# Two transformer layers on one core: the first layer's modulation, routing and order of work rebuilt

## The chip, the cores and the metric

The kernel runs on one core of a Trainium2 chip. The metric is the time of one execution on the device in microseconds (us): the median of three runs is 1533.65, the lowest 1533.04, the highest 1539.41. A core has five engines with instruction streams of their own: PE (matrix products; the profile shows its weight loads as PEld), DVE (vector), ACT (activation functions), POOL (GpSimd, which also issues the indirect DMAs) and SP (which issues most plain DMAs). They meet at semaphores.

## What is computed

Two layers over x of 4 batches x 1024 tokens x 256 features, all in float32. Each layer takes six modulation vectors per batch from a small product, `silu(c) @ wmod`.

```
mod = silu(c) @ wmod                 -> sa, ca, ga, sb, cb, gb   (per batch; ga, gb kept away from 0)
x = x + ga * attn(layernorm(x) * (1 + ca) + sa)
x = x + gb * ffn (layernorm(x) * (1 + cb) + sb)
```

In the first layer `attn` is attention without softmax, so it can be written with the 256x256 gram matrix of a batch's rows: h times (masked gram, combiners, queries). Its `ffn` is a mixture of eight experts (256 -> 1024 -> 256, relu). A router (256 -> 8) picks the two best experts of each token, and their outputs are added with softmax weights. The second layer has a gated MLP whose weights decay from chunk to chunk, and a second mixture of eight experts.

## The kernel before

A tile is 128 tokens; a batch has NC = 8 tiles. The program has three stages.

1. **Attention and routing of the first layer**, batch by batch (lines 509 to 638). `modulation` (L177) makes the six vectors and spreads them over all partitions by products with a selector (L214) and copies. `attention_in(b)` normalises eight tiles (`normalise`, L225: statistics on DVE at L231, a square root on ACT at L236, the rows on ACT at L247), multiplies by the scale on DVE (L522), adds the shift on POOL (L523), transposes four tiles at a time on PE (`transpose4`, L256; evicted on ACT at L257), and forms the gram matrix (L546) and the small head products (L556, L568) that give a 128x128 masked matrix `md`. `attention_out` (L589) multiplies and adds to x on DVE (L597). `route0` normalises again, modulates, transposes, makes the router's logits (L617), stores the rows to DRAM, and calls `top2` and `Group.add`.
2. **The experts** (L641 to L728). The 8192 (token, expert) pairs are sorted by expert and cut into J = 71 blocks of 128. For each block POOL gathers the expert's weight rows (nothing moves where the expert stays the same) and the 128 input rows `xg`; PE transposes them (L655), multiplies by W1 (L671), ACT applies the relu (L678), PE multiplies by W2 (L690), DVE adds the bias (L698), SP stores the block to y0. At block 4 the second layer's modulation is made (again L188, L214, L221, L222).
3. **The second layer** (L731 on), chunk by chunk.

**The pair table.** `Group.add` ranks each pair within its expert (two float16 products, L368 and L369) and builds, for each of a tile's two choices, a 128x128 one-hot table scaled by the token's number (`g_at`, L391). `Group.close` counts the blocks of each expert, and 64 products of `g_at` with a one-hot over blocks (`g_which`, L472; L479) add up to the table `row`, which says which token stands at each place of each block. `wrow` holds the weight rows of a block, with an out-of-range number where the expert is the one already there.

**The order of the work.** A scheduler orders each engine's instructions at compile time from estimated costs; the source order only ranks them. Tiles live in pools with a fixed number of buffers, and an instruction waits for its buffer's last reader. The PSUM pools are `ps_1` (3 buffers), `ps_2` (2) and `ps_m` (3). The indirect DMAs stand in POOL's stream (L499), the plain ones in SP's or ACT's.

Of the kernel before, what the change touches and what calls it, by code (L numbers as in the profile page):

```python
# [8 lines left out]
F32 = mybir.dt.float32  # L9
# [4 lines left out]
AX = mybir.AxisListType  # L14
PSUM = bass.MemoryType.PSUM
DRAM = bass.MemoryType.DRAM

P = 128
# [19 lines left out]
def adaln_d2_kernel(  # L38
# [46 lines left out]
    nc.scalar.dma_start(c0, c0T)  # L85

    def load_x(b):
        nc.sync.dma_start(x_sb[:, :, b, :], x_in[b].rearrange("(c p) d -> p c d", p=P))

    load_x(0)  # L90

    poolA = tc.tile_pool(name="poolA", bufs=2)
    pa = poolA.__enter__()

    def load_mod(pool, wmod):
        w = pool.tile([P, KD, 6 * D], F32, name="wmod", bufs=1)
        for piece in range(3):
            cut = slice(piece * 2 * D, (piece + 1) * 2 * D)
            nc.scalar.dma_start(
                w[:, :, cut], wmod[:, cut].rearrange("(k p) n -> p k n", p=P)  # L100
            )
        return w

    wm0 = load_mod(pa, wmod0)
    qT = pa.tile([P, KD, 4, 64], F32, name="qT", bufs=1)
    comb = pa.tile([P, KD, 4, 64], F32, name="comb", bufs=1)
    load_x(1)
    nc.scalar.dma_start(comb, comb_in)
    nc.scalar.dma_start(qT, qT_in)
    load_x(2)  # L110
    load_x(3)
    wr_sb = const.tile([P, KD, E], F32, name="wr_sb")
    rw_sb = const.tile([P, KD, E], F32, name="rw_sb")
    br_sb = const.tile([P, E], F32, name="br_sb")
    for dst, src in ((wr_sb, WrT), (rw_sb, rwT), (c1, c1T)):
        nc.scalar.dma_start(dst, src)
    nc.scalar.dma_start(br_sb, br.partition_broadcast(P))
# [42 lines left out]
    def iota(name, pattern, shape, base=0, mult=0):  # L160
        i = const.tile(shape, I32, name=f"{name}_i")
        nc.gpsimd.iota(i, pattern=pattern, base=base, channel_multiplier=mult)
        f = const.tile(shape, F32, name=name)
        nc.gpsimd.tensor_copy(f, i)
        return f
# [5 lines left out]
    steps = iota("steps", [[P, NC * B]], [P, NC * B])  # L171

    token0 = iota("token0", [[P, NC * B]], [P, NC * B], base=-2048, mult=1)
# [3 lines left out]
    def modulation(scratch, layer, cT, w, names):  # L177

        sT = small.tile([P, KD, B], F32, name=f"sT{layer}")
        nc.scalar.activation(sT, cT, AF.Silu)  # L180
        rows = scratch.tile([B, 6, D], F32, name="mod_rows", bufs=1)
        tiles = []
        for i, (where, name) in enumerate(names):
            tiles.append(where.tile([P, B, D], F32, name=f"{name}{layer}", bufs=1))
        for piece in range(3):
            pr = psum(ps_m, [B, 2, D], "pm_mod")
            for k in range(KD):
                nc.tensor.matmul(  # L188
                    pr,
                    lhsT=sT[:, k, :],  # L190
                    rhs=w[:, k, piece * 2 * D : (piece + 1) * 2 * D],
                    start=(k == 0),
                    stop=(k == KD - 1),
                )
            for i in range(2):
                kind = (2 * piece + i) % 3
                dst = rows[:, 2 * piece + i, :]
                if kind == 0:
                    nc.scalar.copy(dst, pr[:, i, :])
                elif kind == 1:  # L200
                    nc.vector.tensor_scalar(dst, pr[:, i, :], 1.0, None, ALU.add)
                else:

                    sign = scratch.tile([B, D], F32, name="g_sign", bufs=1)
                    nc.vector.tensor_scalar(sign, pr[:, i, :], 0.0, 2.0, ALU.is_ge, ALU.mult)
                    size = scratch.tile([B, D], F32, name="g_size", bufs=1)
                    nc.vector.scalar_tensor_tensor(
                        size, sign, -1.0, pr[:, i, :], ALU.add, ALU.mult
                    )
                    nc.vector.tensor_scalar(size, size, 0.25, None, ALU.max)  # L210
                    nc.vector.scalar_tensor_tensor(dst, sign, -1.0, size, ALU.add, ALU.mult)
            for b in range(B):
                pb = psum(ps_m, [P, 2, D], "pm_bc")
                nc.tensor.matmul(  # L214
                    pb,
                    lhsT=pick[:, b, :],
                    rhs=rows[:, 2 * piece : 2 * piece + 2, :],
                    start=True,
                    stop=True,
                )  # L220
                nc.scalar.copy(tiles[2 * piece][:, b, :], pb[:, 0, :])  # L221
                nc.vector.tensor_copy(tiles[2 * piece + 1][:, b, :], pb[:, 1, :])  # L222
        return tiles
# [274 lines left out]
    def gather(dst, table, index, bound=None):  # L498
        nc.gpsimd.indirect_dma_start(  # L499
# [8 lines left out]

    gb0_pool = const
    sha0, sca0, ga0, shb0, scb0, gb0 = modulation(  # L510
        pa,
        0,
        c0,
        wm0,
        [(pa, "sha"), (pa, "sca"), (pa, "ga"), (pa, "shb"), (pa, "scb"), (gb0_pool, "gb")],
    )
    g0 = Group(const, "g0", NC * B, token0, pa)
    rows0 = dram.tile([B * NC * P, D], F32, name="rows0")
    hT_of = {}

# [4 lines left out]
    def attention_in(b):  # L525
        h = pa.tile([P, NC, D], F32, tag="h", name="h1")
        hT = pa.tile([P, KD, NC, P], F32, tag="hT", name="h1T")
        hT_of[b] = hT
        normalise([x_sb[:, c, b, :] for c in range(NC)], [h[:, c, :] for c in range(NC)])
        for g in range(NC // 4):  # L530
            cs = slice(4 * g, 4 * g + 4)
            modulate(
                h[:, cs, :],
                sca0[:, b, :].unsqueeze(1).to_broadcast([P, 4, D]),
                sha0[:, b, :].unsqueeze(1).to_broadcast([P, 4, D]),
            )
            transpose4(
                [h[:, c, :] for c in range(4 * g, 4 * g + 4)],
                lambda k: hT[:, k, cs, :],
            )  # L540

        gram = psum(ps_1, [P, KD, P], "pm_gram")
        for j in range(KD):
            for c in range(NC):
                hj = h[:, c, j * P : (j + 1) * P]
                nc.tensor.matmul(  # L546
                    gram[:, j, :], lhsT=hj, rhs=hj, start=(c == 0), stop=(c == NC - 1)
                )
        gd = pa.tile([P, KD, P], F32, tag="gd", name="gd")
        nc.gpsimd.memset(gd, 0.0)  # L550
        for r in (slice(0, 64), slice(64, P)):
            nc.vector.tensor_copy(gd[r, :, r], gram[r, :, r])
        t1 = pa.tile([P, KD, 4, 64], F32, name="t1")
        for j in range(KD):
            p1 = psum(ps_1, [P, 4 * 64], "pm_t1")
            nc.tensor.matmul(  # L556
                p1,
# [5 lines left out]
            nc.scalar.copy(t1[:, j, :, :].rearrange("p a g -> p (a g)"), p1)  # L563
# [12 lines left out]
        md = pa.tile([P, KD, P], F32, tag="md", name="md")  # L576
        nc.gpsimd.memset(md, 0.0)
# [3 lines left out]
        return md  # L581

    def attention_out(b, md):
        hT = hT_of[b]
        for c2 in range(NC // 2):
# [13 lines left out]
    def route0(b):  # L599
        h = pa.tile([P, NC, D], F32, tag="h", name="h2")  # L600
        hT = pa.tile([P, KD, NC, P], F32, tag="hT", name="h2T")
        normalise([x_sb[:, c, b, :] for c in range(NC)], [h[:, c, :] for c in range(NC)])
        pl = psum(ps_1, [P, NC, E], "pm_l")
        for g in range(NC // 4):
            cs = slice(4 * g, 4 * g + 4)
            modulate(
                h[:, cs, :],
                scb0[:, b, :].unsqueeze(1).to_broadcast([P, 4, D]),
                shb0[:, b, :].unsqueeze(1).to_broadcast([P, 4, D]),
            )  # L610
            transpose4(
                [h[:, c, :] for c in range(4 * g, 4 * g + 4)],
                lambda k: hT[:, k, cs, :],
            )
            for c in range(4 * g, 4 * g + 4):
                for k in range(KD):
                    nc.tensor.matmul(  # L617
                        pl[:, c, :],
                        lhsT=hT[:, k, c, :],
                        rhs=wr_sb[:, k, :],  # L620
                        start=(k == 0),
                        stop=(k == KD - 1),
                    )
        nc.sync.dma_start(
            rows0[b * NC * P : (b + 1) * NC * P, :].rearrange("(c p) d -> p c d", p=P), h
        )
        cut = slice(b * NC, (b + 1) * NC)
        top2(pl, br_sb, NC, g0.one[:, :, cut, :], g0.w[:, :, cut], None)
        g0.add(b * NC, NC)

    mds = {0: attention_in(0)}
    for b in range(B):
        if b + 1 < B:
            mds[b + 1] = attention_in(b + 1)
        attention_out(b, mds[b])
        route0(b)
    g0.close(2048, True)
# [10 lines left out]

    def fetch(work, table, index):
# [383 lines left out]
```

## Time and profile before

| quantity | value |
|---|---|
| median of three runs | 1533.65 us |
| the profiled execution | 1540.93 us, its span (first to last instruction) 1539.2 us |
| mean granted PE clock | 0.878 of full speed |
| busy time of PE, DVE, ACT, POOL | 1219.2, 536.8, 514.8, 611.5 us |
| first product of an expert | 234.7 us from the span's start |
| last expert block's add (L698) | 786.4 us |
| indirect DMAs of expert weights (L499, w) | 142, 994 ns each on POOL |

How to read a profile line: start, duration, engine, line of the kernel, operation, output <- inputs, shape, how many were merged, and in brackets how long the engine had been idle and what released it. In the list of windows, each engine has its busy time and, in brackets, its number of instructions. Products in float32 appear as two records, transposes as one.

### The profile page before, as it was taken

The page shows a single profiled execution, that of the slowest core. Times are in us where ns is not written, and L with a number is a line of the kernel's source. Part 1 is how long each engine was busy: PE and PEld are TensorE (multiplying, and loading weights), DVE is VectorE, ACT ScalarE, POOL GpSimd, SP SyncE. Part 2 cuts the span into 40 slices and gives each one's busy share as a digit, 9 for nine tenths or more (in the row PEclk, how much of TensorE's full clock was granted, in tenths as well). Part 3 has the DMA queues.
Part 4 walks back from the last instruction along what each step waited for, and adds up shares of the span by engine and source line. Part 5 has one row for each costly group of instructions (what it writes and reads, how often), then busy time and mean ns, then how long its engine had stood idle before and what let it go on. Part 6 is the DMA issues. An engine that isn't in the chain of part 4 may idle for free.

```text
span 1539.2 us, 17629 instructions
## 1 busy us (share of the span) xinstructions
PE 1219.2 (79%) x6137; PEld 920.1 (60%) x6137; DVE 536.8 (35%) x1719; ACT 514.8 (33%) x1153; POOL 611.5 (40%) x592
## 2 busy tenths in 40 slices
PE   4966449999999999999940679999988898724683
PEld 1566438599989999899930345565545464513341
DVE  5487560210101001100115645555652425152143
ACT  3254203234344443344322315544251423121121
POOL 3022213143334333443347841111244433687645
PEclk8766559799999999999975889999999999856786
DMA  7000024043242332414122210000124332535633
GB/s 281 1 28 28 30 70 171 14 151 112 77 152 65 127 119 67 155 38 152 32 59 72 69 34 14 14 14 1 39 62 129 92 100 76 153 113 166 169 114 101
DMA packets 81048, 133.18 MB, mean 87 GB/s; under 512 B 25760, under 2 KB 60704, under 8 KB 76864
## 3 DMA queue, kind: packets, MB, share of 16 engines
q0 software_dynamic: 38576, 83.90, 18.5%
q1 hardware_dynamic: 39744, 44.45, 8.4%
q10 hardware_dynamic: 2640, 3.70, 0.7%
q8 instruction: 49, 0.80, 0.2%
q14 instruction: 39, 0.32, 0.1%
HBM read 228.66 MB, written 30.54 MB: 168 GB/s over the span
## 4 chain that ended last, share of the span: by engine, by line
PE 49%; POOL 12%; issue 10%; DMA 10%; DVE 7%; ACT 3%; POOLq 0%; DVEq 0%; ACTq 0%
PE p_h L671 14%; PE p_y L690 13%; PE p_f L796 6%; POOL yg L499 5%; PE p_u L781 3%; DMA w<-in_W,g_wrow 3%; PE p_v L781 3%; DMA we<-in_ew,ga_wrow 2%; PE p_e L879 2%; DMA we<-in_ew,gb_wrow 2%; POOL h L523 2%; POOL x_sb L756 2%; POOL xg L499 2%; PE pm_x L655 1%; PE pm_t L256 1%
## 5 line engine op out<-in xcount | busy, mean ns | idle before, releaser
L678 ACT ACTIVATE hid<-p_h,w 128x128 f32<-128x128 f32 x568 | 208.2, 367 | 341.8 <-PE p_h L671 322.8
L671 PEld LDWEIGHTS p_h<-xT,w 128*128 128x128 f32 x2272 | 298.0, 193 | 19.9 <-DVE xT L657 6.7
L690 PE MATMUL p_y<-w,hid 128*128 128x256 f32 x1136 | 299.7, 381 | 5.3 <-DMA w<-in_W,g_wrow 5.3
L671 PE MATMUL p_h<-xT,w 128*128 128x128 f32 x2272 | 303.1, 277 | 0.6 <-DVE xT L657 0.5
L499 POOL DMA_INDIRECT w<-in_W,g_wrow x142 | 141.1, 994 | 326.7 <-ACT hid L678 228.8
L690 PEld LDWEIGHTS p_y<-w,hid 128*128 128x128 f32 x1136 | 192.2, 192 | 22.1 <-DMA w<-in_W,g_wrow 3.8
L698 DVE TENSOR_TENSOR y<-p_y,w 128x256 f32<-128x256 f32 x71 | 30.2, 425 | 466.6 <-PE p_y L690 460.3
L879 PE MATMUL p_e<-we,xT 128*128 128x256 f32 x280 | 91.4, 462 | 78.1 <-DMA we<-in_ew,gb_wrow 43.9
L781 PE MATMUL p_v<-h3T,a 128*128 128x512 f32 x256 | 131.6, 628 | 15.2 <-ACT hf L789 15.2
L781 PE MATMUL p_u<-h3T,a 128*128 128x512 f32 x256 | 130.5, 624 | 4.6 <-DVE hf L790 3.8
L879 PEld LDWEIGHTS p_e<-we,xT 128*128 128x128 f32 x280 | 58.5, 227 | 112.6 <-issue 49.5
L256 PE MATMUL pm_t<-ident,h 128*128 128x128 f32 x256 | 45.0, 331 | 90.4 <-POOL h L523 90.2
L796 PE MATMUL p_f<-a,hf 128*128 128x256 f32 x512 | 114.4, 382 | 0.0
L796 PEld LDWEIGHTS p_f<-a,hf 128*128 128x128 f32 x512 | 97.7, 192 | 17.5 <-issue 4.5
L657 DVE COPY xT<-pm_x 128x256 f32<-128x256 f32 x141 | 56.3, 419 | 143.6 <-PE p_e L879 113.3
L256 PEld LDWEIGHTS pm_t<-ident,h 128*128 128x128 f32 x256 | 37.0, 175 | 102.0 <-POOL h L523 99.7
L781 PEld LDWEIGHTS p_v<-h3T,a 128*128 128x128 f32 x256 | 48.4, 200 | 68.1 <-issue 43.6
L499 POOL DMA_INDIRECT xg<-rows,g_row x71 | 68.4, 963 | 50.0 <-PE pm_x L655 22.5
L523 POOL TENSOR_TENSOR h<-h,shb 128x1024 f32<-128x1024 f32 x16 | 38.4, 2399 | 115.2 <-DVE h L522 85.0
L781 PEld LDWEIGHTS p_u<-h3T,a 128*128 128x128 f32 x256 | 48.8, 200 | 55.7 <-issue 42.9
L887 ACT COPY y<-p_e 128x256 f32<-128x256 f32 x70 | 26.0, 371 | 159.4 <-PE p_e L879 156.4
L499 POOL DMA_INDIRECT yg<-y,g_slot x64 | 66.1, 1033 | 32.7 <-issue 29.0
(228 smaller groups left out, 1527.2 us busy)
## 6 DMA issues: line engine op xcount, KB each, us to landing
y<-y SPq DMA_DIRECT2D x71, 128.0 KB, 1.7
ga_y<-y SPq DMA_DIRECT2D x39, 128.0 KB, 2.1
x_sb<-in_x SPq DMA_DIRECT2D x4, 1024.0 KB, 13.1
rows<-h SPq DMA_DIRECT2D x4, 1024.0 KB, 4.5
out_x<-x_sb SPq DMA_DIRECT2D x8, 512.0 KB, 2.9
gb_y<-y SPq DMA_DIRECT2D x31, 128.0 KB, 2.2
wmod<-in_wmod ACTq DMA_DIRECT2D x6, 512.0 KB, 9.4
a<-in_fw SPq DMA_DIRECT2D x3, 1024.0 KB, 10.9
```

The source lines that it names most:

```text
L256: nc.tensor.transpose(pt[:, i, :], src[i][:, k * P : (k + 1) * P], ident)
L499: nc.gpsimd.indirect_dma_start(out=dst, out_offset=None, in_=table, in_offset=bass.IndirectOffsetOnAxis(ap=index, axis=0), bounds_check=bound,
L523: nc.gpsimd.tensor_tensor(h, h, shift, ALU.add)
L657: nc.vector.tensor_copy(xT, pt)
L671: nc.tensor.matmul(p1[:, i, :], lhsT=w1[:, k * H + m * P : k * H + (m + 1) * P], rhs=xT[:, k, :], start=(k == 0), stop=(k == KD - 1),)
L678: nc.scalar.activation(hid[:, m, :], p1[:, i, :], AF.Relu, bias=w1[:, KD * H + m : KD * H + m + 1],)
L690: nc.tensor.matmul(p2, lhsT=hid[:, m, :], rhs=w2[:, m * D : (m + 1) * D], start=(m == 0), stop=(m == KH - 1),)
L698: nc.vector.tensor_tensor(y, p2, w2[:, KH * D :], ALU.add)
L756: nc.gpsimd.tensor_tensor(x_sb[:, c, :, :], x_sb[:, c, :, :], sum_, ALU.add)
L781: nc.tensor.matmul(ps, lhsT=a[:, k, m * P : (m + 1) * P], rhs=hT[:, k, :, :], start=(k == 0), stop=(k == KD - 1),)
L796: nc.tensor.matmul(p2, lhsT=hid[m][:, b * P : (b + 1) * P], rhs=a1[:, m, :], start=(m == 0), stop=(m == KH - 1),)
L879: nc.tensor.matmul(p2, lhsT=xT[:, k, :], rhs=we[:, k * D : (k + 1) * D], start=(k == 0), stop=(k == KD - 1),)
```

## The change

It rewrites the first stage and touches the other two only where they take something from it.

- **Modulation at the eviction.** The shift and scale of the first layer are made with features on the partitions (`mods_by_feature`). The normalised rows are transposed first; ACT's eviction of the transposes applies scale and shift as per-partition operands (`to_features`). Where token-major rows are needed (gram, rows in DRAM), PE transposes back and ACT copies (`to_tokens`). The multiply on DVE and the add on POOL are gone.
- **Pair numbers by indirect DMA.** The class `Regions` takes the place of `Group` in the first layer. Each expert has a region of 4096 places in a DRAM table. After a batch is ranked, one indirect DMA per tile and choice writes 128 pair numbers of 4 bytes to their places: 64 DMAs in all. At the end one gather of 71 lines of 128 numbers reads the table back in blocks. It waits for all the scatters. `g_at`, `g_which` and their products are gone. The softmax weights and slots are computed later, at block 4 of the experts (`weights`).
- **A fixed order.** Inside `tc.manual_schedule` the instructions of PE, ACT, DVE and POOL keep the source order, and the source weaves the first attention half of batch b+1 into the second half of batch b. The last batch is routed in two halves. x is loaded in halves.
- **The second layer's modulation** is multiplied out at the end of the first stage (`modulation1`) and spread at expert block J-8 (`spread1`).
- **Rows two blocks ahead.** `xg` of block j+2 is gathered ahead of the weights of block j.

The core of the diff (`-` before, `+` after):

```
+    def to_features(b, src, n0, dst, d0, shift, scale):
+        for k in range(KD):
+            pt = psum(ps_m, [P, 4, P], "pm_t")
+            for i in range(4):
+                nc.tensor.transpose(pt[:, i, :], src[:, n0 + i, k * P : (k + 1) * P], ident)
+            nc.scalar.activation(dst[:, k, d0 : d0 + 4, :], pt, AF.Identity,
+                bias=modT[:, shift, k, b : b + 1], scale=modT[:, scale, k, b : b + 1])
...
+        def scatter(self, s):
+            for i in range(2):
+                nc.gpsimd.indirect_dma_start(
+                    out=self.table.rearrange("r l -> (r l)").unsqueeze(1),
+                    out_offset=bass.IndirectOffsetOnAxis(ap=self.index[:, i, s : s + 1], axis=0),
+                    in_=self.pair[:, i, s : s + 1], ...)
...
-    mds = {0: attention_in(0)}
-    for b in range(B):
-        if b + 1 < B:
-            mds[b + 1] = attention_in(b + 1)
-        attention_out(b, mds[b])
-        route0(b)
-    g0.close(2048, True)
+    with tc.manual_schedule(engines=ORDERED):
...
+        for b in range(B):
+            last = b == B - 1
+            for g in range(2):
+                attention_out(b, g)
+                if b and g:
+                    g0.ranks()
+                norm2(b, g)
+                if not last:
+                    features1(b + 1, g)
+                if b and g:
+                    g0.places()
+                    for q in range(2):
+                        scatter(b - 1, q)
+                if not last:
+                    tokens1(b + 1, g)
+            if not last:
+                gram(b + 1)
+                pl = psum(ps_1, [P, NC, E], "pm_l")
+                features2(b, 0)
+                t1 = head_t1(b + 1)
+                router(b, 0, pl[:, :4, :])
+                features2(b, 1)
+                head_m(b + 1, t1)
+                tokens2(b, 0)
+                router(b, 1, pl[:, 4:, :])
+                if b + 2 < B:
+                    for g in range(2):
+                        norm1(b + 2, g)
+                tokens2(b, 1)
+                g0.route(pl, br_sb, b * NC, NC)
+            else:
+                sT1 = silu_of(1, c1)
+                for g in range(2):
+                    features2(b, g)
+                    pl = psum(ps_1, [P, 4, E], "pm_l")
+                    router(b, g, pl)
+                    if g:
+                        g0.ranks()
+                        g0.places()
+                        scatter(b, 0)
+                    tokens2(b, g)
+                    g0.route(pl, br_sb, b * NC + 4 * g, 4)
+                modulation1(sT1, wm1, 0)
+                g0.ranks()
+                g0.places()
+                scatter(b, 1)
+                g0.total()
+                modulation1(sT1, wm1, 1)
+                g0.close(pa, lambda: modulation1(sT1, wm1, 2))
...
     def expert_in(j):
         w1 = w1buf[j % 2]
+        if j + 2 < g0.J:
+            xg_of[j + 2] = rows_of(work, rows0, g0.row[:, j + 2 : j + 3])
         gather(w1, W1, g0.wrow[:, j : j + 1], E * P - 1)
         gather(w2buf[j % 2], W2, g0.wrow[:, j : j + 1], E * P - 1)
-        xT = fetch(work, rows0, g0.row[:, j : j + 1])
+        xT = turned(work, xg_of.pop(j))
...
         if j == 4:
-            sha1, sca1, ga1, shb1, scb1, gb1 = modulation(work, 1, c1, wm1, ...)
+            g0.weights(work)
+            for i in (2, 5):
+                gate_of(rows1[:, i, :], rows1[:, i, :], work)
+        if j == g0.J - 8:
+            sha1, sca1, ga1, shb1, scb1, gb1 = spread1(l1)
```

The functions named in the loop: `attention_out(b, g)` the products of half a batch with `md` and the add to x; `norm1` and `norm2` the normalisation of half a batch (four tiles) for attention and for routing, without modulation; `features1` and `features2` call `to_features`; `tokens1` and `tokens2` call `to_tokens`, the latter also stores the rows; `gram`, `head_t1` and `head_m` the parts of the old `attention_in`; `route` the two best experts; `ranks` up to nine float16 products; `places` the place numbers from them.

## The prediction

> **What bounds it now.** I read the page's slices first, to see which stage belongs to which part of the program, then the chain that ended last for the stage's end, then the windows and the time line inside it. Times are microseconds from the span's start.
>
> ```profile
> PE   4966449999999999999940679999988898724683
> ...
> PEclk8766559799999999999975889999999999856786
> ```
>
> A slice is 38.5 us. Six uneven slices hold the first layer's attention and routing; then PE is full for fourteen, in all but one at a granted clock of 0.9 or more (the 71 expert blocks, to 786.4); the second layer follows. The diff leaves the second layer's instructions in the same order on all engines, so I cost it at nothing. What is at stake is when the experts start, and what the experts lose on the way. The chain at the seam:
>
> ```profile
> 218.62 6.35 issue
> 225.01 0.51 issue
> 225.55 0.19 issue
> 225.73 7.73 DMA xg<-rows,g_row
> 233.55 0.68 PE pm_x L655 x2
> 234.25 0.44 DVE xT L657
> 234.73 2.93 PE p_h L671 x12
> ```
>
> The pair table is closed, the first rows are gathered (7.73, beside 5 MB of weight loads issued at 224.7), and at **234.7** the experts begin. Inside the stage no engine is full for long:
>
> ```profile
> core 0: us, PE busy (x) PEld busy (x) DVE busy (x) ACT busy (x) POOL busy (x), PEclk, DMA share, GB/s
> 75.00:100.00 25.00, 16.14 (x72) 14.86 (x72) 20.72 (x71) 13.40 (x25) 7.37 (x4) 0.62 0.13 43
> 100.00:125.00 25.00, 17.63 (x116) 15.97 (x116) 21.52 (x81) 10.13 (x21) 7.87 (x3) 0.77 0.08 26
> 125.00:150.00 25.00, 15.32 (x81) 14.35 (x80) 18.63 (x71) 9.75 (x18) 4.68 (x2) 0.64 0.05 17
> ```
>
> DVE leads with 21 of 25, PE runs at 0.62 to 0.77 of its clock, and a batch takes (200.0 - 98.0)/3 = 34 (the first DVE instruction on the router's logits, batch 0 to batch 3).
>
> **What goes and what comes, per batch.** Gone: DVE's multiply by the scale (27.6 in all) and POOL's add of the shift (40.1), the tables g_at (14.6) and g_which (10.0) on DVE, 64 table products on PE, eight loads of activation tables at 1.28. New: 32 more transposes a batch on PE with 8 evictions, and 16 scatters on POOL. By busy time the batch gets lighter on DVE (about 21). But the order is now fixed on PE, ACT, DVE and POOL, and it is the order that I cost. One batch, from the residual add of its first half to the next batch's:
>
> - A. Two residual adds 1.4, statistics to first normalised row 3.6 (four pairs at 0.39, a square root 0.21, then five dependent DVE steps at 0.2), four ACT rows 2.0, and only then the two evictions of the *next* batch's transposes, which ACT holds behind them (128x512 with a pointer scale, nearest row 0.68): 8.4. PE waits for these evictions.
> - B. Eight transposes back to tokens, 16 output products, an add: 3.6 at full clock (1.07 + 1.85 + 0.7), 6.4 at half (1.97 + 3.78 + 0.7).
> - C. The same normalisation for the second half: 7.0.
> - D. Transposes and 32 gram products: 4.9 or 9.3.
> - E. Features 1.07, the tail of their eviction 0.7, router 1.9, features 1.07, head product 1.06, the masked product on DVE 0.7: 6.5, or 10.7 with the products at half.
> - F. DVE then normalises two halves of the batch after next, the second behind ACT's rows of the first (7.2), and routes, 13 steps at 0.25 (3.3): 10.5, and the next residual add is queued behind it.
>
> The sum is 40.9 at full clock and 52.3 at half. Here the time line decides:
>
> ```profile
> 115.32 3.49 PE L589 MATMUL pm_o<-md,h1T 128*128 128x128 f32 x16 [2.90 <-DVE md L580]
> 119.92 1.09 PE L256 MATMUL pm_t<-ident,h 128*128 128x128 f32 x8 [1.11 <-POOL h L523]
> ```
>
> After a wait of 2.90, 16 products take 3.49 (half); soon after, 8 transposes take 1.09 (full). With A and C a batch has two PE waits of over 5, so I take slightly more half than full: **47.2** for two batches; the third has no later batch to normalise, and F is the rest of the router and the routing, 5.6 or 8.2: 36.0 to 50.0, taken 43.7.
>
> The Trainium skill, page "TensorE: Matmul & The Clock Gate", section "What's actually happening", says that an idle window of about 3.4 us halves the clock and 3.4 us of sustained work restores it. By that rule two halves are each followed by 3.4 us at half, and the batch would be 40.9 + 3.4 = 44.3. The trace differs: 14 router products at 125.92 took 2.99, half clock, with no wait over 1.11 in the six microseconds before.
>
> **The prologue.** SP's queue gets the input in halves, the table's fill behind the expert weights, and the row stores in halves; nothing waits for these near its end. ACT issues its loads until 14.8, as now. Two table loads (2.56), the root and DVE's steps: first rows at 19.3. DVE waits for the feature-wise modulation (16 small products at 0.22) before the second half's statistics; its rows end at 26.2 and the first evictions, again queued behind them, at 27.6. Back-transposes, gate rows, gram, head and 4 spreads lead to the masked product at 50, two normalisations of batch 1 on DVE (7) stand before the first residual add: 57 (53 to 62). Batch 3's adds: 57 + 2 x 47.2 + 43.7 = **195.1**.
>
> **The tail.** From there, adds and two normalisations on DVE 9.7 and the places of batch 2, 1.3: scatters can start after 11.0. 32 remain (16 of batch 2, 8 + 8 of batch 3), all on POOL. No scatter is in the trace; the nearest row, an indirect gather with 128 indices:
>
> ```profile
> 789.73 0.96 POOL L499 DMA_INDIRECT yg<-y,g_slot  x1 [12.33 <-issue]
> 791.00 0.96 POOL L499 DMA_INDIRECT yg<-y,g_slot  x1 [0.30 <-issue]
> ```
>
> One each 1.27. Bounds: 0.95 (its duration without the gap) and 1.89 (the slowest of that run of gathers, 1.59 + 0.30, beside DVE work); it can't be hidden by the last batch, whose places are ready 32 after the adds while POOL is busy to 51.6. I take 1.27: 32 x 1.27 = 40.6 (30.4 to 60.5). Behind it on POOL: a weight gather 1.3, wait for the last scatter and issue 1.5, the pair table's landing 3.0, two DVE steps, a transpose and a copy 1.3, three row gathers (PE transposes three blocks before its first product) 2.5 + 2.9 landing, products 0.6: 12.0. If the 5 MB of weights collide with them again, 4.8 more. Experts start at 195.1 + 11.0 + 40.6 + 12.0 = **258.7**, which is 24.0 later than 234.7.
>
> The Trainium skill, page "DMA: Bandwidth & Descriptors", section "Specifications", says that transfers under 512 bytes make the DMA engine read, modify and write; a scatter writes 4 bytes per descriptor. It speaks against this change, no row here shows such a write, and the page gives no time for it; the sum stands without it.
>
> **In the experts.** The second layer's modulation leaves block 4's place. Block ends at 254.75 and 311.63 hold four blocks, 56.9 instead of 4 x 7.28 = 29.1: 27.8 lost.
>
> ```profile
> 272.72 4.59 PE L214 MATMUL pm_bc<-mod_rows,pick 4*128 4x512 f32 x8
> 277.24 3.58 PE L188 MATMUL pm_mod<-wmod,sT 128*4 128x512 f32 x4
> 280.75 3.13 PE L690 MATMUL p_y<-w,hid 128*128 128x256 f32 x10
> 283.81 3.69 PE L214 MATMUL pm_bc<-mod_rows,pick 4*128 4x512 f32 x8
> ```
>
> The spreads come back near the end, 24 records in one stretch, 10.4 (0.43 each) to 20.7 (0.86 at half); taken 15.5. Gain 12.3 (7.1 to 17.4). The row products run under the scatters at no cost; without that cover, three times four records at 0.86, 10. Slots and weights at block 4 lie in DVE's 6.5 idle per block. Gathering rows two blocks ahead gains nothing: PE waits only 5.3 in the whole expert stage, all for weights, and POOL needs 3.9 of 7.28 a block.
>
> **Sum.** +24.0 - 12.3 = +11.7. The profiled execution took 1540.9 (span 1539.2, 1.7 outside) and would take 1552.6; the median of the runs is 1533.65, 7.3 below, and from it I get **1545**.
>
> **Rivals.** About 0.5% (7.7 us, 1526 to 1541) is what the measurement can tell from no change.
>
> 1. *Faster: the denser PE keeps its clock.* All batches at full clock: 57 + 2 x 40.9 + 36.0 = 174.8, experts at 238.4 (+3.7), spreads at full (-17.4): 1520. For: more transposes fill PE. Against: A and C leave PE idle twice a batch. It decides when batch 3's adds come before 176 (181 if the spreads run full). Chance 0.20.
> 2. *No difference: POOL is not the bound.* Scatters at 0.95: 10.2 less, 1535. For: the bare duration. Against: 0.30 stands before every one in the row. Chance 0.20.
> 3. *Clearly slower: scatters at 1.89*, or the half clock all along (T at 57 + 104.6 + 50.0 = 211.6): +20 or +16, 1561 to 1565. For: DVE beside POOL, tiny writes. Chance 0.20.
> 4. The forecast, 1545 (1540 to 1555), 0.40.
>
> The range takes in rivals 1 and 3: **1520 to 1566**. Faster is rival 1, 0.20; the same is rival 2 and the forecast's lower edge, 0.23; slower the rest, 0.57.
>
> **What would show it.** After: expert start near 259; two PE waits of over 5 a batch, released by ACT's evictions; 32 indirect issues on POOL back to back ahead of the first expert gather; no modulation gap at blocks 4 and 5. A batch period under 42, scatters far from 1.27, or POOL idle before the last eight would prove me wrong.

## The result and the profile after

| quantity | before | after |
|---|---|---|
| median (4 runs each) | 1536.53 us | 1611.42 us |
| ratio, 95% interval | 1 | 1.049 (1.041 to 1.057) |
| the profiled execution (span) | 1540.93 (1539.2) | 1621.79 (1620.0) |
| first product of an expert | 234.7 | 325.0 |
| last expert block's add | 786.4 | 873.0 |

The change costs 75 us; the forecast was 1545 with a range to 1566. The slices of the page show where: PE's full stretch begins after eight slices of 40.5 us instead of after six, and the last two ahead of it hold next to nothing (2 and 0 tenths).

```profile
PE   4656552099999999999995077999997989643683
...
PEclk9676756599999999999888578999999999975887
```

The chain at the seam, which ended at 234.73 before:

```profile
236.50 23.36 DMA g_table<-pair,g_index
...
278.94 27.68 DMA g_table<-pair,g_index x2
306.69 0.66 issue
307.38 0.22 issue
307.60 5.20 DMA g_pairs<-g_table,g_line
...
318.32 6.17 DMA xg<-rows,g_row
324.54 0.69 PE pm_x L1082 x2
325.23 2.56 PE p_h L1100 x12
```

Two waits for scatters (the writes of pair numbers) make up 51 us of it. The last scatter was issued at 287.88 and the gather of the pair table (`g_pairs`) could not go before 307.60. The forecast had counted POOL's time for issuing a scatter; what ends last here is not the issue but the landing. POOL itself stands between the last 32 scatters, twice for about 8 us:

```profile
248.85 0.97 POOL L671 DMA_INDIRECT g_table<-pair,g_index  x1 [8.83 <-DMA g_table<-pair,g_index]
...
272.56 0.97 POOL L671 DMA_INDIRECT g_table<-pair,g_index  x1 [7.91 <-DMA g_table<-pair,g_index]
...
307.60 1.88 POOL L541 DMA_INDIRECT g_pairs<-g_table,g_line  x1 [17.18 <-DMA g_table<-pair,g_index]
```

The windows of the stage, in the columns of before (each engine's busy time and, in brackets, its instructions):

```profile
75.00:100.00 25.00, 19.18 (x144) 17.60 (x144) 8.22 (x39) 11.88 (x22) 0.00 (x0) 0.86 0.06 22
100.00:125.00 25.00, 9.10 (x52) 7.87 (x53) 12.00 (x49) 11.47 (x23) 3.02 (x3) 0.66 0.07 22
125.00:150.00 25.00, 17.86 (x122) 16.04 (x122) 3.12 (x12) 5.25 (x9) 9.83 (x11) 0.70 0.02 1
...
275.00:300.00 25.00, 0.00 (x0) 0.00 (x0) 0.00 (x0) 0.00 (x0) 11.74 (x12) 0.50 0.01 0
```

DVE falls from 21 busy of 25 to 8, 12 and 3. In the last window POOL issues scatters, the other engines do nothing, and the DMA share is 0.01.

There is a second loss, inside the batches. From one batch's first residual add to the next took 44.4, then 56.6, then 54.8 (58.49, 102.85, 159.49, 214.24). The time line at the first place where they lengthen:

```profile
133.08 0.97 POOL L671 DMA_INDIRECT g_table<-pair,g_index  x1 [0.30 <-issue]
135.17 0.73 PE L921 MATMUL pm_m<-t,qT 128*64 128x64 f32 x16
140.51 0.45 PE L869 MATMUL pm_b<-ident,h2T 128*128 128x128 f32 x1
144.98 0.97 POOL L671 DMA_INDIRECT g_table<-pair,g_index  x1 [10.93 <-issue]
146.15 0.83 PE L869 MATMUL pm_b<-ident,h2T 128*128 128x128 f32 x3 [5.18 <-issue]
147.27 0.59 DVE L932 TENSOR_TENSOR md<-pm_m,ga 64x128 f32<-64x128 f32 x2 [16.03 <-PE pm_b L869]
```

The head products `pm_m` end at 135.90 and DVE, which has nothing else to do, multiplies them by the gate at 147.27: a hand-over of 11.37, where the same pair of instructions took 0.11 in the batch before. PE stands still for 5.18 in the middle of a group of four transposes, POOL for 10.93 after ten scatters in a row. All this is while scatters are in flight. (A hand-over, here and below, is the time from the end of the products to the start of the instruction on another engine that needs them.)

### The profile page after: what moved, and what is told of

The parts are those of the page before. It is cut to its first block, busy times and chain, and to the rows that moved or that the text cites. A ratio compares the mean times of both kernels' runs of the same rounds, so it can differ in the third digit from the quotient of the medians.

```text
span 1620.0 us, 17869 instructions
## 1 busy us (share of the span) xinstructions
PE 1219.1 (75%) x6245; PEld 929.2 (57%) x6245; DVE 482.6 (30%) x1576; ACT 528.9 (33%) x1177; POOL 634.2 (39%) x639
## 4 chain that ended last, share of the span: by engine, by line
PE 47%; DMA 15%; issue 13%; POOL 12%; DVE 8%; ACT 4%; POOLq 0%; SPq 0%; ACTq 0%; DVEq 0%
PE p_h L1100 12%; PE p_y L1119 11%; PE p_f L1223 6%; POOL yg L541 4%; DMA w<-in_W,g_wrow 3%; PE p_u L1208 3%; DMA g_table<-pair,g_index 3%; DMA we<-in_ew,ga_wrow 3%; PE p_v L1208 3%; PE p_e L1306 2%; POOL xg L541 2%; DMA we<-in_ew,gb_wrow 2%; POOL x_sb L1183 2%; PE pm_bc L214 2%; POOL h L552 1%
## 5 line engine op out<-in xcount | busy, mean ns | idle before, releaser
L1100 PEld LDWEIGHTS p_h<-xT,w 128*128 128x128 f32 x2272 | 299.9, 194 | 18.8 <-DVE xT L1084 4.6
L1100 PE MATMUL p_h<-xT,w 128*128 128x128 f32 x2272 | 303.8, 277 | 0.2 <-DVE xT L1084 0.2
L671 POOL DMA_INDIRECT g_table<-pair,g_index x64 | 62.4, 975 | 220.3 <-DVE g_index L664 135.0
L1306 PE MATMUL p_e<-we,xT 128*128 128x256 f32 x280 | 87.5, 449 | 73.2 <-DMA we<-in_ew,gb_wrow 42.6
L1208 PEld LDWEIGHTS p_v<-h3T,a 128*128 128x128 f32 x256 | 48.6, 201 | 68.3 <-issue 44.3
L1208 PEld LDWEIGHTS p_u<-h3T,a 128*128 128x128 f32 x256 | 48.3, 198 | 55.4 <-issue 42.6
L1082 PE MATMUL pm_x<-ident,xg 128*128 128x128 f32 x282 | 53.4, 295 | 30.9 <-DMA xg<-ga_rows,ga_row 11.3
L298 PE MATMUL pm_t<-ident,h 128*128 128x128 f32 x128 | 19.2, 297 | 70.5 <-POOL h L552 70.1
## 6 DMA issues: line engine op xcount, KB each, us to landing
x_sb<-in_x SPq DMA_DIRECT2D x8, 512.0 KB, 10.9
rows<-h SPq DMA_DIRECT2D x8, 512.0 KB, 11.7
```

Of the source, the lines that this page charges most:

```text
L671: nc.gpsimd.indirect_dma_start(out=self.table.rearrange("r l -> (r l)").unsqueeze(1), out_offset=bass.IndirectOffsetOnAxis(ap=self.index[: ...
L1082: nc.tensor.transpose(pt[:, k, :], xg[:, k * P : (k + 1) * P], ident)
L1100: nc.tensor.matmul(p1[:, i, :], lhsT=w1[:, k * H + m * P : k * H + (m + 1) * P], rhs=xT[:, k, :], start=(k == 0), stop=(k == KD - 1),)
L1208: nc.tensor.matmul(ps, lhsT=a[:, k, m * P : (m + 1) * P], rhs=hT[:, k, :, :], start=(k == 0), stop=(k == KD - 1),)
L1306: nc.tensor.matmul(p2, lhsT=xT[:, k, :], rhs=we[:, k * D : (k + 1) * D], start=(k == 0), stop=(k == KD - 1),)
```

## The experiments

The times are those of one profiled execution where no interval stands. "Experts start" is the first product of L1100; the run of the kernel before on the same chip stands in brackets.

**1. No scatters at all** (the pair table keeps its fill).

```
     def scatter(b, g):
-        for i in range(4):
-            g0.scatter(b * NC + 4 * g + i)
+        pass
```

> All 64 scatters are left out; the pair table keeps its fill, so the rows gathered are not the right ones, and all other instructions stand. In the changed kernel the first expert product starts at 325.2. Theory A (the DMA engines finish a scatter's 128 four-byte writes only every 2.6 us or so: 13 issued from 272.6 on had landed at 306.7, (306.7 - 272.6)/13; from the first scatter at 121 on, everything that goes through the DMA engines waits in line behind them): the stalls at 141.0 (5.2) and 196.7 (13.8) vanish, all three batch periods are near the first one's 44.4, batch 3's adds come at 58.5 + 3 x 44.4 = 192, and the experts start at 192 + 11 + 12 = 215 (210 to 225). Rival B (POOL's issue at 1.27 is the bound, as forecast): the periods stay at 57 and 61, only the tail of about 40 goes, start near 285. Rival C (the fixed order itself makes the periods long): start above 240 with both stalls still there.

Measured: experts start at 237.8, run 1539.10 (1535.25). The periods are 45.0, 44.5 and 39.1, and both stalls are gone, as theory A has it. The start is 23 later than theory A's 215, outside its range, for a reason of the sum: it left out that the last places are known only 29 after batch 3's adds (184.0 to 213.35), a wait that the scatters used to cover, and that the first rows land in 9.37.

```profile
213.18 0.17 DVE g_index L664
...
217.38 5.23 DMA g_pairs<-g_table,g_line
...
228.13 9.37 DMA xg<-rows,g_row
```

So rival C (the order itself makes the periods long) falls, and B with it. But the run says one thing more: with the storing of pairs left out altogether, the new stage ends 3.1 *later* than the old one with its whole pair table (one execution of each). These 3 us are no price of the new stage, though. Where the pair table keeps its fill, the kernel turns every entry into row 0, so a gather reads one and the same row 128 times; the first rows then land in 8.8 to 9.4 (experiments 1, 2, 3, 6, 9 and 10), against 6.1 to 6.9 in the four kernels that gather the right rows (the changed one and experiments 5, 7 and 8). Without that the two stages would end about level (an estimate from these landings): the fixed order and the modulation at the eviction win nothing by themselves.

**2 and 3. The same number of scatters, each pair in a row of its own 512 bytes**, once 4 bytes of it (the edit shown), once all 512.

```
-            nc.vector.tensor_copy(self.index[:, :, cut], self.pos[:, :, cut])
+            nc.vector.tensor_scalar(self.index[:, :, cut], self.pos[:, :, cut], 128.0, None, ALU.mult)
...
-                        out=self.table.rearrange("r l -> (r l)").unsqueeze(1),
+                        out=self.apart.rearrange("r l -> (r l)").unsqueeze(1),     # [E*n*P, 128] in DRAM
```

> The same 64 scatters of four bytes a pair, but each pair number goes to a row of its own, 512 bytes from its neighbour, in a table beside; the pair table keeps its fill, so the rows gathered are not the right ones. Theory A1 (the cost is that of a small write, wherever it goes): 2.6 us a scatter as now, experts start at 315 to 330. Theory A2 (the cost is that up to 16 neighbouring places of one expert lie in the same 64 bytes and are written one after the other): scatters land as fast as POOL issues them, no stalls, 215 + the tail of 32 scatters at 1.27 = 255 (245 to 265).

> As the one before, with 512 bytes written per pair (128 times as much data) into a row of its own; the pair table keeps its fill. Theory A1 with the reason that a write under 512 bytes is read, modified and written: whole 512-byte rows land fast, the start falls to about 255 (245 to 265). Theory A1 with the reason that every descriptor of a scatter costs the same whatever its size: 315 to 330 or later. Theory A2: 245 to 265 too; it is told from the first reason by the kernel before.

Measured: experts start at 260.7 and 257.4, runs 1557.43 and 1554.66 (1535.25). The 3 us between the two stand already at the first residual add (58.4 and 55.3), ahead of all scatters (in all these kernels it comes either at 55.3 to 55.5 or at 58.0 to 58.5), so 4 bytes and 512 cost the same. Theory A2 holds: it is not the small write that costs, but small writes beside each other. In the kernel with 4 bytes POOL runs without a stop, from the first of the last 32 scatters to the gather that reads the table:

```profile
197.56 0.97 POOL L672 DMA_INDIRECT g_apart<-pair,g_index  x1 [11.20 <-DVE g_seen L666]
...
237.29 0.97 POOL L672 DMA_INDIRECT g_apart<-pair,g_index  x1 [0.30 <-issue]
238.56 1.05 POOL L541 DMA_INDIRECT w<-in_W,g_wrow  x1 [0.30 <-issue]
240.49 1.88 POOL L541 DMA_INDIRECT g_pairs<-g_table,g_line  x1 [0.88 <-issue]
```

and the hand-over that took 11.37 is back to 0.04 (PE's products end at 136.33):

```profile
135.60 0.73 PE L922 MATMUL pm_m<-t,qT 128*64 128x64 f32 x16
136.37 0.59 DVE L933 TENSOR_TENSOR md<-pm_m,ga 64x128 f32<-64x128 f32 x2 [4.70 <-PE pm_m L922]
```

**4. Half the scatters** (first choices only: `for i in range(1)`).

> Only the scatters of the first choices, 32 of 64; the pair numbers of the second choices are left out, so some rows gathered are not the right ones. Theory A: half the writes, so the drain behind the last 16 scatters is 16 x 2.6 = 42 instead of 83, and the stalls of 5.2 and 13.8 vanish: 325 - 42 - 19 = 264 (250 to 280). Rival B (POOL's issue): 16 scatters of 1.27 fewer in the tail, 325 - 20 = 305.

Measured: start 252.1, run 1559.76 (1535.25). The price goes with the writes, not with POOL's issue (which would leave 305); one long hand-over, 5.18, is left.

**5 and 6. How far apart is apart?** First the changed kernel itself, with each block's 128 places turned so that neighbours lie 68 bytes apart in the block's 512 (scatter and slots alike); then 4 bytes at every 64 in a table beside, which is the edit of experiment 2 with 16 for 128.

```
+            nc.vector.tensor_scalar(far, self.pos[:, :, cut], 17.0, None, ALU.mult)
+            nc.vector.tensor_scalar(far, far, P - 1, None, ALU.bitwise_and)
+            nc.vector.tensor_copy(own, self.pos[:, :, cut])
+            nc.vector.tensor_scalar(own, own, E * self.size - P, None, ALU.bitwise_and)
+            nc.vector.tensor_tensor(self.index[:, :, cut], own, far, ALU.add)
+            nc.vector.tensor_copy(self.pos[:, :, cut], self.index[:, :, cut])
```

> The changed kernel with every pair's place p inside its block of 128 turned to (17 x p) mod 128, for the scatter and for the slots alike: the table is as dense as before, but of the 16 or so pairs that one scatter writes for one expert no longer all fall on neighbouring words; they fall 68 bytes apart, two in each 64 bytes of the block's 512. Five small DVE instructions more a batch. Theory A2 (neighbouring words are what costs) with pieces of 64 bytes as the unit: the scatters go at POOL's pace as in the kernel with rows 512 bytes apart, experts start at 261 + 1 to 3 = 263, run about 1558 to 1562. A2 with 512 bytes as the unit: nothing changes, 325 and 1611.

> Four bytes a pair, 64 bytes from the neighbour, in a table beside (the pair table keeps its fill, so the rows gathered are not the right ones). A2 with a unit of 64 bytes: 261 as at 512 bytes. A2 with a unit of 512 bytes (8 neighbours in one unit instead of 16): the drain falls by about half, 325 - 32 to 40 and one stall less, 275 to 290.

Measured: starts 296.4 and 286.0; the turned kernel 1599.33, ratio to before 1.034 (1.029 to 1.039); the other 1590.66 (1547.54). The first lies between the two answers that I had written down, the second in that for a unit of 512 bytes: 64 bytes between neighbours are not enough, and less is paid than with neighbouring words. At 64 bytes POOL no longer stands, but the hand-overs still do: 2.52 after the gram products here (they end at 126.14), 6.18 a batch later.

```profile
121.07 5.07 PE L896 MATMUL pm_gram<-h 128*128 128x128 f32 x32
128.66 0.59 DVE L900 COPY gd<-pm_gram 64x128 f32<-64x128 f32 x2 [11.68 <-remote]
```

**7. All scatters late, first try** (all 64 calls moved behind the last places in the source).

> All 64 scatters as in the changed kernel, neighbouring words, but issued only when the last places are known (213.4 without any scatter), so that no row store, no batch and nothing else runs beside them. Theory A2: the batches run as without scatters (last residual adds at 190), and the drain is 64 x 2.6 = 166: the experts start at 213.4 + 166 + 20.4 (from there to the first product without scatters: 237.8 - 217.4) = 400 (385 to 415). Rival: the price of 2.6 belongs to the row stores and other traffic beside, alone a scatter goes at POOL's 1.27: 213.4 + 81 + 20.4 = 315.

This did not do what it was meant to: start 334.9, run 1638.96 (1547.54), and the first scatter still goes out at 117.2. POOL has nothing else in that stretch, so a scatter runs when its own places are known, wherever it stands in the source. It is the changed kernel once more, 10 us later (325.0 there) and with a longest hand-over of 18.71 instead of 15.74; so much the same writes differ from one kernel to the next.

**8. All scatters late, by data.** The pair numbers are copied once, after the last places, and the scatters write the copy.

```
+                nc.vector.tensor_copy(g0.pair, g0.pair0)      # pair_late, after the last places()
+                for s in range(B * NC):
+                    g0.scatter(s)
```

> In the kernel with late issue all scatters still ran as soon as their places were there, since POOL had nothing else to wait for. Here the pair numbers that they write are copied (one DVE instruction of 128x64) only after the last places, so all 64 wait for it, neighbouring words as in the changed kernel. A2: no scatter in flight during the batches, so the hand-over from the gram products to DVE's copy stays at 0.04 in all four batches and the last residual adds come near 190; then 64 x 2.6 = 166 with nothing beside: experts at 213.6 + 166 + 20.4 = 400 (385 to 415). Rival (the price of a scatter comes from row stores and instructions beside it): 213.6 + 64 x 1.27 + 20.4 = 315.

Measured: start 377.4, run 1674.49 (1538.03). Batches as without scatters (55.3, 100.6, 145.1, 184.2), all eight hand-overs between 0.04 and 0.14. Then 64 scatters from 214.05 to the last landing at 359.4: **2.27 us each**, with nothing beside them; a little less than the 2.6 that I had, so the start lies below my 385 to 415. The rival is out: the price is the scatter's own. The line's listing, and the same listing for experiment 2:

```profile
L672 POOL DMA_INDIRECT g_table<-pair_late,g_index x64: 971/972/1187, 214.1 to 350.9; - x64
...
DMA to landing us min/median/max: 8.7/16.5/25.2
```

```profile
L672 POOL DMA_INDIRECT g_apart<-pair,g_index x64: 970/972/1184, 121.8 to 237.3; - x64
...
DMA to landing us min/median/max: 2.1/2.1/3.6
```

On POOL both take 0.972; from issue to landing one takes 2.1, the other 16.5 (at one every 2.27 that is some seven in flight).

**9 and 10. The unit from two more sides**: 64 bytes written whole, densely; and 4 bytes at every 256 (edits as in 2 and 3, with a row of 16 words, and with 64 for 128).

> Like the kernel with four bytes at every 64, but all 64 bytes are written (16 words a pair), densely, no piece of 64 bytes by two pairs; beside the pair table, which keeps its fill. If a write is only slow because it fills part of a 64-byte piece: 257 to 263 as with whole 512-byte rows. If 512 bytes are the unit, in which several writes collide: as the kernel with four bytes at every 64, 286 (275 to 295), PE to DVE hand-overs of several us.

> Four bytes a pair, 256 bytes from the neighbour (table beside, pair table keeps its fill). With 512 bytes as the unit two neighbours collide instead of eight: 257 to 270, a hand-over now and then above 0.04. With a unit of 256 bytes or less: 257 to 261 and 0.04 everywhere.

Measured: starts 259.9 and 260.2, runs 1557.05 and 1558.31 (1538.03), landings of 2.1 in both. The table of all:

| written per pair, every | landing (median) | longest hand-over | experts start |
|---|---|---|---|
| 4 B, 4 B (the change) | 16.5 (experiment 8) | 15.74 | 325.0 |
| 4 B, 68 B within 512 | - | 8.71 | 296.4 |
| 4 B, 64 B | - | 6.18 | 286.0 |
| 64 B, 64 B | 2.1 | 0.04 | 259.9 |
| 4 B, 256 B | 2.1 | 0.04 | 260.2 |
| 4 B, 512 B | 2.1 | 0.04 | 260.7 |
| 512 B, 512 B | 2.2 | 0.04 | 257.4 |

(Hand-over: from the end of the gram or head products to DVE's first instruction on them, from the first scatter on. In the two rows without a landing the trace pairs no issue of a scatter with its landing.) Scattered writes of 4 bytes are slow when the next one lies 4 or 64 bytes away, and not at 256; 64 bytes written whole, side by side, are not slow. The rows "4 B, 64 B" and "64 B, 64 B" write to the same places of a table of the same size, so the size of the table is not the cause. If pieces of memory that several writes share are what costs, as theory A2 has it, they would have to be larger than 64 and at most 256 bytes; why whole 64 bytes are then free was not tested.

**11 and 12. The part of the change that gains, put on the kernel before.** The second layer's modulation rows are multiplied ahead of `close`, where PE waits for DVE; the twelve spreads come back one in each of twelve blocks; the 5 MB of second-layer weights wait for an expert block's result.

```
+    rows1_products()                       # 12 products, to rows1
     g0.close(2048, True)
...
+        if j == 7:                         # second version: 1
+            for t in (a0, a1, a2, ew):     # their loads wait for y of this block
+                nc.vector.tensor_copy(<first element of t>, y[:, 0:1])
...
         if j == 4:
-            sha1, ... = modulation(work, 1, c1, wm1, ...)
+            rows1_finish(work)
+        if j >= 10 and j % 4 == 2 and (j - 10) // 4 < 12:      # second version: 11 and 3
+            spread1(mods1, (j - 10) // 4 % 3, (j - 10) // 12)
```

> The kernel before with one part of the change alone, and further: the second layer's modulation rows are multiplied ahead of the pair table's closing, where PE waits for DVE; the spreads come back one each in twelve blocks between 10 and 54; and the 5 MB of weight loads wait for block 7's result instead of running beside the first gathered rows. No pair scatter, no fixed order. Blocks 3 and 4 took 13.53 and 27.71 before, 26.7 over two blocks of 7.28; twelve spreads of two records at 0.59 (full clock) cost 14, at 1.06 they cost 25. Gain 12 to 2 there, and 4.8 at the first gathered rows (7.73 against 2.9): 1535 - 17 = 1518, at worst 1528. Rival: PE pays for the rows and spreads wherever they stand: 1530 to 1535.

> The kernel before with the second layer's modulation rows ahead of the pair table's closing and the twelve spreads one each in blocks 11, 15, ... 55 (in the earlier version blocks 10 and 50 were also blocks in which an expert's weights change, and took 13.3 and 13.2), and the 5 MB of weight loads behind block 1's result instead of block 7's. Two collisions of about 6 go: 0.9965 x 1535 = 1530, minus 10 to 12: 1518 to 1522, a ratio of 0.990. Rival: a spread costs PE 1.3 to 2 wherever it stands and the collisions move to other blocks: 0.995 to 0.997.

Measured: 1542.05, ratio 0.9965 (0.9941 to 0.9989), a third of what was expected; then 1524.28, ratio **0.990** (0.987 to 0.994), as expected. In the first, blocks 10 and 50 took 13.33 and 13.22, blocks with a spread in which an expert's weights change as well (block 10 comes shortly after the 5 MB, and PE waits 4.19 for weights there). The second moves the spreads and the 5 MB away from them; no block then takes over 8.75, but the two moves were not tried apart. The first rows land in 2.9 instead of 7.73 in both versions. The second is faster than both kernels, by 1% than the one before.

## Why the prediction was wrong

Each step of the sum, with what the changed kernel and the kernel of experiment 2 (rows 512 bytes apart) show:

| step | forecast | changed | rows apart |
|---|---|---|---|
| first residual add | 57 | 58.5 | 58.4 |
| batch 3's adds | 195.1 | 214.2 | 186.7 |
| to the first of the last 32 scatters | 11.0 | 12.0 | 10.9 |
| 32 scatters (changed: to the last landing; rows apart: to the end of the last issue) | 40.6 | 80.4 | 40.7 |
| from there to the experts | 12.0 | 18.3 | 22.4 |
| experts start | 258.7 | 325.0 | 260.7 |

- **The step that failed** is the tail's "32 x 1.27 = 40.6 (30.4 to 60.5)", with POOL as the bound. POOL's part was right: 1.27 apart where it runs, and 40.7 in all when the rows lie apart. But the bounds were both taken from what POOL spends on an indirect *gather* (and the 1.59 in the upper one was not the slowest: in the kernel before, the gather of the same line at 864.25 took 1.98); a scatter's landing was put at one wait of 1.5 at the end. On neighbouring words a scatter lands every 2.27 alone and every 2.5 here (226.28 to 306.69 for 32). That is +39.8 of the miss of 66.3.
- **The page that spoke against the change was cited and left out of the sum.** The Trainium skill, page "DMA: Bandwidth & Descriptors", section "Specifications", puts a read-modify-write under transfers of less than 512 bytes. Experiments 2 and 3 show no price for the small write alone (4 and 512 bytes in rows apart land in 2.1 and 2.2); several such writes near each other cost 2.27 a scatter. Rival 3 had "tiny writes" as its reason, but at POOL's 1.89, so its 1561 to 1565 was too low as well.
- **That scatters in flight slow all engines was in no rival.** Batch 3's adds came 19.1 late, by the stalls at 141 and 197 (5.18 and 13.83 on PE). With the rows apart they come 8.4 *early*: the periods are 44.8, 44.5 and 39.0, not 47.2, 47.2 and 43.7. My mix of slightly more half clock than full was too dark; the 44.3 that the prediction worked out from the page "TensorE: Matmul & The Clock Gate", section "What's actually happening", was nearer. Half clock stood where the prediction had it, behind the two waits (16 output products in 3.09 at 113.12 in experiment 2), and the products of step E ran at full clock (16 router products in 1.85 at 137.20).
- **The rest of the tail** took 18.3 and 22.4 instead of 12.0: the pair table lands in 5.1 to 5.2 (forecast 3.0), the rows in 6.2 and 9.0 (2.9; of the 9.0 some 3 come from gathering one row 128 times). The 5 MB of weights are issued beside them again, for which I had 4.8 as a possibility only. And the terms listed for the 12.0 add up to 13.1. In the kernel with rows apart this error and the early batches cancel; its 260.7 against 258.7 is partly luck.
- **In the experts** 12.3 was to be gained; from the first product to the last add it is 551.7 before, 548.0 after: 3.7. The spreads stand in one stretch and take 27.09 for a block of 7.28, so 19.8, near the top of my 10.4 to 20.7. Blocks 4 and 5 had lost 26.7 before (13.53 and 27.71), so 6.9 are won there; 3.2 are lost in the other blocks, which was not followed further. (DVE's adds at the end of two blocks:)

```profile
798.96 0.42 DVE L1127 TENSOR_TENSOR y<-p_y,w 128x256 f32<-128x256 f32 x1 [6.60 <-PE p_y L1119]
826.05 0.42 DVE L1127 TENSOR_TENSOR y<-p_y,w 128x256 f32<-128x256 f32 x1 [8.84 <-PE p_y L1119]
```

  The same 24 records cost 0.928 each there, 0.640 when spread over twelve blocks (experiment 12); the groups of the changed kernel, then of that one:

```profile
L214 PE MATMUL pm_bc<-rows,pick 4*128 4x512 f32 x24 | 18.1, 928 | 0.0
```

```profile
L257 PE MATMUL pm_bc<-rows,pick 4*128 4x512 f32 x24 | 13.4, 640 | 0.0
```

  In the one stretch PE is never idle, and yet its granted clock (third number from the end) is 0.50:

```profile
804.00:818.00 14.00, 14.00 (x21) 5.90 (x20) 3.72 (x9) 2.86 (x8) 0.96 (x1) 0.50 0.00 0
```

- **Right:** slower; the two PE waits a batch behind ACT's evictions (7.22 and 6.04 at 110.6 and 123.0); rows two blocks ahead gain nothing (PE waits 6.9 in the experts' second products, all for weights); no gap at blocks 4 and 5. **Two of the signs I had given for being wrong** are what the trace shows: scatters far from 1.27 (2.5 each to the landing), and POOL idle (8.83 and 7.91 within the last 32; the second ahead of the last thirteen, not of the last eight). The 32 issues do not stand back to back.

So the 90.3 by which the experts start later are 3.1 for the new stage without any scatter (237.8 - 234.7), 22.9 for 64 scatters at POOL's pace (260.7 - 237.8), and 64.3 for writing them side by side (325.0 - 260.7). Each is good to 3 us only: the 3.1 are the gathers of one row, of the 22.9 some 3.0 stand at the first residual add already (58.4 against 55.4), and the 64.3 would be some 3 more with the right rows in experiment 2. After the experts' last add the changed kernel is 5.8 shorter (747.0 against 752.8) with the same instructions in the same order; in experiments 1 to 10 that stage takes 746.6 to 755.3, so this is within what one kernel differs from the next.

## What to carry to other kernels

Cost a scatter by when it lands and by where its writes lie, not by the time that POOL takes to issue it: here a scatter of 128 numbers of 4 bytes to neighbouring words landed every 2.27 us against 1.27 at the issue, and the same numbers 256 bytes apart were free behind it. When all engines stand at once and the DMA share is near nothing, look for many small writes in flight. And put work that is moved off a seam into blocks where nothing else collides: one spread in each of twelve blocks cost a third less on PE (0.640 against 0.928 a record) than twelve in a row.

## What the hardware showed that was not expected

- Hand-overs between engines depend on what the DMA engines are writing. With scatters on neighbouring words in flight, DVE began up to 15.74 us after the PE products that it needs (18.71 in experiment 7); without, 0.04 to 0.14. It is the signal that is late: the trace keeps the time of every semaphore update, and for the head products that end at 135.90 PE's update stands at 147.25 and DVE starts at 147.27, while in experiment 2 the end is at 136.33, the update at 136.35 and DVE's start at 136.37. Between 134 and 217 in the changed kernel 21 of PE's updates come 0.6 to 16.0 after the end of their products; all earlier ones come within 0.02, and so do all up to 240 in experiments 1, 2, 3, 8, 9 and 10. What holds the signals up was not tried. PE's own stops (5.18 and 13.83) begin with four and five of its updates outstanding; whether they have the same cause, or whether PE lacks instructions, is open too (the profile lists a DMA queue q8 of kind `instruction`; a packet of it at 184.47 took 2.96 in the changed kernel, none over 1.38 in experiment 1).
- Plain stores pay too: the 512 KB row stores land in 11.7 (median) beside dense scatters, in 2.9 beside the scatters of experiment 2. From the lists of DMA issues of the changed kernel, then of that one:

```profile
rows<-h SPq DMA_DIRECT2D x8, 512.0 KB, 11.7
```

```profile
rows<-h SPq DMA_DIRECT2D x8, 512.0 KB, 2.9
```

- POOL issues about ten slow scatters and then stands until some have landed (ten from 121.37 to 133.08, the next at 144.98). The ten are the program's: its indirect DMAs go round eight semaphores, and the eleventh waits on the one that the third had.
- A scatter of 4 bytes a row, rows 512 bytes apart, lands in 2.1. The Trainium skill, page "DMA: Bandwidth & Descriptors", section "Anatomy of one DMA — SWDGE (gpsimd) path", puts a fixed part of about 2.0 on a DMA, most of it the wait for the target memory's receipt; that agrees.
